# Selective scan with its states dealt out as a Latin square, and a quarter of du*B made by TensorE and ScalarE

## The chip, the core and the metric

The kernel runs on one core of a Trainium2 chip. A core has several engines, each with its own instruction stream, worked off in program order: TensorE (PE in the profile) multiplies matrices into PSUM, VectorE (DVE) and GpSimd (POOL) work elementwise, ScalarE (ACT) evaluates `func(scale * x + bias)`, and SyncE (SP) issues transfers (DMA) between the chip's memory and the on-chip memory SBUF. The engines meet only through semaphores: an instruction starts when what it reads has been written and what it overwrites has been read.

The metric is the device time of one execution in microseconds. The time before is 8235.37 us, the median of three runs (8234.65 to 8238.02).

## The reference

Two layers over images of 128 channels and 128 x 128 pixels, four of them, in float32. The first is a Mamba block over the L = 16384 pixels of an image as a sequence, the second a filter in the frequency domain. The change is in the first, around its recurrence:

```python
u     = silu(conv(x_in) + conv_b)                 # 256 channels
dt, Bm, Cm = split(u @ x_proj_w.T, [8, 24])       # 8, 16 and 16 columns
delta = softplus(dt @ dt_proj_w.T + dt_proj_b)    # 256 channels
A     = -exp(A_log)                               # 256 channels x 16 states

def step(h, inp):                                 # over the 16384 pixels
    d_t, B_t, C_t, u_t = inp
    dA = exp(d_t[:, :, None] * A)
    h  = h * dA + d_t[:, :, None] * B_t[:, None, :] * u_t[:, :, None]
    y  = einsum('bds,bs->bd', h, C_t)
    return h, y

y = (ys + u * D) * silu(z)
out = y @ out_proj_w.T                            # then group norm, silu, + x
```

There are 256 x 16 = 4096 recurrences per image, each over 16384 steps: h = h * dA + du*B, where du is delta * u. After it come a group normalisation with Silu and the residual, a small pooled network that yields four weights per image, and the second layer.

## The kernel before

**Chunks, units, pairs.** A chunk k is T = 512 pixels of one image; there are 4 x 32 = 128. A partition holds one channel and one of four states: 32 channels (DG) x 4 states (SQ) = 128 partitions. A chunk's recurrences are then 2 halves of channels (j, 128 channels each) x 4 groups of states (g) x 4 groups of channels in the half (m), 32 tiles of 128 x 512. A unit is four of these tiles: before, one (j, g) with all four m. A unit is worked in two pairs, so a chunk has NP = 16 pairs.

**Loads.** B, C, delta and du come out of the chip's memory in that layout: B and C by repeating four rows of states over 32 channels, delta and du by repeating every channel over four states.

```python
def bc_load():
    for q, tag in enumerate("BC"):
        t = d[tag] = p2.tile([P, NG, T], ...)
        for g in range(NG):
            nc.sync.dma_start(out=t[:, g, :],
                in_=d["bc"][q, g * SQ : (g + 1) * SQ, :].partition_broadcast(DG))
def dt_act():                                    # delta, and its store
    delta = d["dn"] = p1.tile([P, NH, T], ...)
    for j in range(NH):
        nc.scalar.activation(delta[:, j, :], ps["dt", j], AF.Softplus, bias=...)
    for j in range(NH):
        nc.sync.dma_start(out=d["dd"][0, j * P : (j + 1) * P, :], in_=delta[:, j, :])
def du_pool(j):                                  # du, and its store
    if j == 0:
        d["dun"] = p1.tile([P, NH, T], ...)
    du = d["dun"][:, j, :]
    nc.gpsimd.tensor_tensor(du, d["dn"][:, j, :], d["u"][:, j, :], ALU.mult)
    nc.sync.dma_start(out=d["dd"][1, j * P : (j + 1) * P, :], in_=du)
```

**The unit.** GpSimd makes du*B for all four tiles in one instruction (`dbu`). ScalarE makes two exponentials per pair into PSUM (`exps`). VectorE scans them; the product with C is VectorE's for most second pairs, GpSimd's for most first pairs (`scans`). TensorE adds the states up into y, one PSUM bank for each half (`sums`).

```python
def dbu(u):
    hb = d["hb", j, g] = p4.tile([P, ND, T], ...)
    nc.gpsimd.tensor_tensor(hb, d["du", j],
        d["B"][:, g : g + 1, :].to_broadcast([P, ND, T]), ALU.mult)
def exps(n):
    da = d["da", j, g, m] = psd.tile([P, 2, T], ...)             # PSUM, 2 buffers
    for q in range(2):
        nc.scalar.activation(da[:, q, :], d["delta", j][:, m + q, :], AF.Exp, scale=...)
def scans(n):
    dve = m > 0 or (j == 0 and g == NG - 1)
    h = da if dve else p2.tile([P, 2, T], tag="h", ...)
    for q in range(2):
        nc.vector.tensor_tensor_scan(h[:, q, :], da[:, q, :], hb[:, m + q, :], init, ALU.mult, ALU.add)
    eng = nc.vector if dve else nc.gpsimd
    eng.tensor_tensor(hb[:, m : m + 2, :], h, cr, ALU.mult)      # cr: C of group g
    nc.scalar.copy(last, h[:, :, T - 1])                         # state for the next chunk
def gate(j):                                                     # in post(k)
    nc.vector.tensor_mul(d["yg"][:, j, :], d["zs"][:, j, :], d["y", j])
```

**The schedule.** It is written by hand: a slot is one pair, and every piece of a chunk has a slot and a phase. Slot 0 is the pair with which a chunk's scans begin, slots below 0 lie in the chunk before, and all pieces of a slot are issued in the order of the phases.

```python
(-9, "pe", load), (-7, "pe", h1_mm), (-6, "act", h1_act), (-5, "pe", xm_mm), (-4, "act", xm_act),
(-3, "pe", z_mm), (-2, "act", z_act), (-1, "pe", cv_mm 0), (0, "pe", cv_mm 1),
(2, "act", silu_act), (3, "pe", xd_mm), (4, "act", xd_act), (5, "pe", dt_mm), (5, "act", bc_load),
(6, "act", dt_act), (7, "pool", du_pool 0), (8, "pool", du_pool 1),
(9, "act", rep_load 0), (16, "pe", rep_load 1),                  # delta and du, repeated
...
(26, "dve", gate 0), (34, "dve", gate 1), (35, "pe", o_mm), (36, "act", o_act), (50, "dve", o_stats)
# these are moved 16 slots forward, as a chunk's inputs are made during the chunk before
# pair n: exps in slot n - 1, scans in n; unit of pair n: dbu in n - 2, sums in n + 3
for phase in ("sums", "pe", "exps", "act", "pool", "dbu", "scans", "dve", "end"):
```

Since the slots are counted modulo 16, gate 0 stands in slot 10 and gate 1 in slot 2 of the following chunk; `cv_mm` (the convolution, 8 accumulating matmuls over two slots) stands in slots 15 and 0.

While one image is scanned, the image before is normalised (slots 2, 7 and 8 of half its chunks) and pooled (slots 4, 7 and 8 of the other half). For the last image both come after the loop, alone, and then the second layer follows.

Of the kernel before, what the change touches and what calls it, by code (L numbers as in the profile page):

```python
# [26 lines left out]
F32 = mybir.dt.float32  # L27
AF = mybir.ActivationFunctionType
ALU = mybir.AluOpType
# [14 lines left out]
def kernel(ctx: ExitStack, tc: tile.TileContext, a: dict, out: bass.AP):  # L44
# [41 lines left out]
    wdt = const("wdt", [R, DI], a["dt_wT"])  # L86
    cwb = const("cwb", [P, KC, DI], a["conv_wT"].partition_broadcast(P))
    bdt = col("dt_b")
# [29 lines left out]
    wck = cpool.tile([P, KC, DI], F32, tag="wck", name="wck")  # L118
    for t in range(KC):
        nc.vector.tensor_mul(wck[:, t, :], win[:, 0:DI], cwb[:, t, :])  # L120

# [15 lines left out]
def block0(tc, s):  # L137
    nc, B, NCH, NH, NS, NG, ND, R, NX, KC, HALO, C, L, NF, DI = (
        s.nc, s.B, s.NCH, s.NH, s.NS, s.NG, s.ND, s.R, s.NX, s.KC, s.HALO, s.C, s.L, s.NF, s.DI,
    )  # L140
    with ExitStack() as ctx:
        def pool(name, bufs, **kw):
# [3 lines left out]
        p2 = pool("p2", 2)  # L146
        p4 = pool("p4", 4)
        tiny = pool("tiny", 2)
        dbc = pool("dbc", 2, space=DRAM)
        dob = pool("dob", 2, space=DRAM)  # L150
        psp = pool("psp", 2, space=PSUM)
        psy = pool("psy", 1, space=PSUM)
        psd = pool("psd", 2, space=PSUM)

# [16 lines left out]
        def pre(k):  # L171
# [7 lines left out]
            def load():  # L179
                xt = d["xt"] = p2.tile([P, T], F32, tag="xt", name=f"xt_{k}")  # L180
                nc.sync.dma_start(out=xt, in_=s.xflat[b, :, i * T : (i + 1) * T])
# [60 lines left out]
            def bc_load():  # L242
                for q, tag in enumerate("BC"):
                    t = d[tag] = p2.tile([P, NG, T], F32, tag=f"r{tag}", name=f"r{tag}_{k}")
                    for g in range(NG):
                        nc.sync.dma_start(
                            out=t[:, g, :], in_=d["bc"][q, g * SQ : (g + 1) * SQ, :].partition_broadcast(DG)
                        )

# [7 lines left out]
            def dt_act():  # L257
# [4 lines left out]
                for j in range(NH):  # L262
                    nc.sync.dma_start(out=d["dd"][0, j * P : (j + 1) * P, :], in_=delta[:, j, :])

            def du_pool(j):
                if j == 0:
                    d["dun"] = p1.tile([P, NH, T], F32, tag="du", name=f"du_{k}")
                du = d["dun"][:, j, :]
                nc.gpsimd.tensor_tensor(du, d["dn"][:, j, :], d["u"][:, j, :], ALU.mult)  # L269
                nc.sync.dma_start(out=d["dd"][1, j * P : (j + 1) * P, :], in_=du)  # L270

            def rep_load(j):
# [8 lines left out]
                (-3, "pe", z_mm), (-2, "act", z_act), (-1, "pe", partial(cv_mm, 0)), (0, "pe", partial(cv_mm, 1)),  # L281
                (2, "act", silu_act), (3, "pe", xd_mm), (4, "act", xd_act), (5, "pe", dt_mm), (5, "act", bc_load),
                (6, "act", dt_act), (7, "pool", partial(du_pool, 0)), (8, "pool", partial(du_pool, 1)),
                (9, "act", partial(rep_load, 0)), (16, "pe", partial(rep_load, 1)),
            ]

        def dbu(u):

            k, r = divmod(u, NH * NG)
            j, g = divmod(r, NG)  # L290
            d = st[k]
            hb = d["hb", j, g] = p4.tile([P, ND, T], F32, tag="hb", name=f"hb_{k}_{j}_{g}")
            nc.gpsimd.tensor_tensor(hb, d["du", j], d["B"][:, g : g + 1, :].to_broadcast([P, ND, T]), ALU.mult)  # L293

        def pair(n):

            k, r = divmod(n, NP)
            u, m = divmod(r, ND // 2)
            j, g = divmod(u, NG)
            return k, j, g, 2 * m  # L300

        def exps(n):
            k, j, g, m = pair(n)
            d = st[k]
            da = d["da", j, g, m] = psd.tile([P, 2, T], F32, tag="da", name=f"da_{k}_{j}_{g}_{m}")
            for q in range(2):
                c = (j * NG + g) * ND + m + q
                nc.scalar.activation(da[:, q, :], d["delta", j][:, m + q, :], AF.Exp, scale=s.amat[:, c : c + 1])  # L308

        def scans(n):  # L310

            k, j, g, m = pair(n)
            d = st[k]
            hb = d["hb", j, g]
            da = d.pop(("da", j, g, m))
            dve = m > 0 or (j == 0 and g == NG - 1)
            last = d["last", j, g, m] = tiny.tile([P, 2], F32, tag=f"st{j}_{g}_{m}", name=f"st_{k}_{j}_{g}_{m}")
            h = da if dve else p2.tile([P, 2, T], F32, tag="h", name=f"h_{k}_{j}_{g}_{m}")
            for q in range(2):
                init = 0.0 if k % NCH == 0 else st[k - 1]["last", j, g, m][:, q : q + 1]  # L320
                nc.vector.tensor_tensor_scan(h[:, q, :], da[:, q, :], hb[:, m + q, :], init, ALU.mult, ALU.add)  # L321
            cr = d["C"][:, g : g + 1, :].to_broadcast([P, 2, T])
            eng = nc.vector if dve else nc.gpsimd
            eng.tensor_tensor(hb[:, m : m + 2, :], h, cr, ALU.mult)  # L324
            nc.scalar.copy(last, h[:, :, T - 1])  # L325

        def sums(u):

            k, r = divmod(u, NH * NG)
            j, g = divmod(r, NG)  # L330
            d = st[k]
            if g == 0:
                y = d["y", j] = psy.tile([P, T], F32, tag=f"y{j}", name=f"y_{k}_{j}")
                nc.tensor.matmul(y, s.diag[:, j, :], d["u"][:, j, :], start=True, stop=False)
            y = d["y", j]
            for q in range(ND):
                nc.tensor.matmul(  # L337
                    y[q * DG : (q + 1) * DG, :], s.sel, d["hb", j, g][:, q, :], start=False, stop=g == NG - 1
                )

        def post(k):

            b, i = divmod(k, NCH)
            d = st[k]

            def gate(j):
                if j == 0:
                    d["yg"] = p1.tile([P, NH, T], F32, tag="yg", name=f"yg_{k}")
                nc.vector.tensor_mul(d["yg"][:, j, :], d["zs"][:, j, :], d["y", j])

            def o_mm():
                d["po"] = psum(f"o_{k}")
                for j in range(NH):
                    nc.tensor.matmul(d["po"], s.wo[:, j, :], d["yg"][:, j, :], start=j == 0, stop=j == NH - 1)  # L354

            def o_act():
                if i == 0:
                    stats[b] = tiny.tile([P, NCH, 6], F32, tag="stats", name=f"stats_{b}")
                    outs[b] = dob.tile([C, L], F32, tag="ob", name=f"ob_{b}")
                d["o"] = p2.tile([P, T], F32, tag="o", name=f"o_{k}")  # L360
                nc.scalar.copy(d["o"], d["po"])
                nc.sync.dma_start(out=outs[b][:, i * T : (i + 1) * T], in_=d["o"])

            def o_stats():
                nc.vector.bn_stats(stats[b][:, i, :], d["o"])
                st.pop(k - 1, None)

            return [
                (26, "dve", partial(gate, 0)), (34, "dve", partial(gate, 1)), (35, "pe", o_mm), (36, "act", o_act),
                (50, "dve", o_stats),  # L370
            ]
# [40 lines left out]
        def finish(b):  # L412
# [12 lines left out]
            def norm_load(i):  # L425
                xr = g["x", i] = p4.tile([P, T], F32, tag="xr", name=f"xr_{b}_{i}")
                o = g["o", i] = p4.tile([P, T], F32, tag="of", name=f"of_{b}_{i}")
                nc.sync.dma_start(out=xr, in_=s.xflat[b, :, i * T : (i + 1) * T])
                nc.sync.dma_start(out=o, in_=outs[b][:, i * T : (i + 1) * T])
# [29 lines left out]
            def agg_load(i):  # L459
                x1 = g["x1", i] = p4.tile([P, T], F32, tag="xr", name=f"x1_{b}_{i}")  # L460
                nc.sync.dma_start(out=x1, in_=s.x1flat[b][:, i * T : (i + 1) * T])
# [40 lines left out]
            for i in range(NCH):  # L502
                c = (2 + i // 2) * NP
                r = i % 2
                todo += [
                    (c - 3 + r, "pe", partial(norm_load, i)), (c + 2, "act", partial(norm_act, i)),
                    (c + 7, "pe", partial(norm_mm, i)), (c + 8, "dve", partial(norm_dve, i)),
                ]
# [22 lines left out]
        for n in range(n_chunks * NP):  # L531
            todo[n - 1, "exps"].append(partial(exps, n))
            todo[n, "scans"].append(partial(scans, n))
            if n % 2 == 0:
# [4 lines left out]
        with tc.manual_schedule():  # L539
            for n in range(min(slots), max(slots) + 1):  # L540
                for phase in ("sums", "pe", "exps", "act", "pool", "dbu", "scans", "dve", "end"):
                    for f in todo[n, phase]:
                        f()
# [196 lines left out]
```

## Time and profile before

The profile is one execution taken by the hardware profiler. Its page gives, for the span of 8235.9 us:

| engine | busy us | share | instructions |
|---|---|---|---|
| VectorE | 7666.4 | 93% | 6640 |
| GpSimd | 7519.2 | 91% | 2500 |
| TensorE, matmuls | 6064.7 | 74% | 20532 |
| ScalarE | 5263.0 | 64% | 9495 |
| transfers, mean of 16 engines | | 46% | |

By stretches of the span, busy microseconds in each:

| stretch, us | VectorE | GpSimd | ScalarE | TensorE | what runs |
|---|---|---|---|---|---|
| 4000 to 5000 | 954 | 970 | 673 | 714 | scan loop |
| 7000 to 7300 | 204 | 156 | 130 | 154 | end of the loop, normalisation of the last image |
| 7500 to 8236 | 713 | 457 | 321 | 716 | second layer |

A row of the page's costliest groups reads: line, engine, operation, output <- inputs by the program's names, partitions x elements of output and input, count | busy us in total, mean ns of one | idle time of the engine just ahead of them, and what ended most of it. In the names, hb is du*B and later h*C, da the exponential, rB, rC, rdu and rdelta the repeated tiles, st the carried state, dd and bc the buffers in the chip's memory. The view of waits has one row for each kind of wait: who waited <- for whom: us in total, how many times, the longest. Matmuls of float32 stand as two records each.

### The profile page before, as it was taken

Reading aid. Unit: us, or ns where it says so; the run is one execution under the profiler, and the core shown is the slowest. Engines: PE = TensorE matmul, PEld = TensorE weight load, DVE = VectorE, ACT = ScalarE, POOL = GpSimd, SP = SyncE. Lnnn points to the kernel's source line nnn. Section 1 sums busy time; section 2 is a strip of 40 time slices with the busy share of each in tenths; the row PEclk is TensorE's granted clock in tenths of the full one; section 3 lists DMA queues with packets and bytes.
Section 4 is the critical chain, followed back from the end, with each engine's and each line's share of the span. In section 5 each row is a group of like instructions: output and inputs, shape, how many; then the busy total and the mean of one; then the engine's idle time right before and its main releaser. Section 6 shows DMA issues by size and latency. Waiting matters only on the chain.

```text
span 8235.9 us, 73103 instructions
## 1 busy us (share of the span) xinstructions
PE 6064.7 (74%) x20532; PEld 2229.5 (27%) x20532; DVE 7666.4 (93%) x6640; ACT 5263.0 (64%) x9495; POOL 7519.2 (91%) x2500
## 2 busy tenths in 40 slices
PE   6677777776777777777777767777777777569999
PEld 1121121111111222221111222221111222138888
DVE  6999999999999999999999999999999999839999
ACT  5666666666666676676666666676666766534444
POOL 7999999999999999999999999999999999716665
PEclk8777777778988878888888888888888888779999
DMA  4444444444454444445454444445454444454443
GB/s 151 141 141 153 144 152 137 146 153 160 163 175 156 168 155 162 147 161 173 153 176 165 152 165 155 160 149 175 163 172 168 151 150 165 135 171 115 115 124 93
DMA packets 838679, 1257.45 MB, mean 153 GB/s; under 512 B 78200, under 2 KB 276864, under 8 KB 838272
## 3 DMA queue, kind: packets, MB, share of 16 engines
q1 hardware_dynamic: 835760, 1252.43, 46.0%
q8 instruction: 162, 2.65, 0.1%
q14 instruction: 245, 2.01, 0.1%
q10 hardware_dynamic: 2512, 0.36, 0.0%
HBM read 1009.22 MB, written 243.27 MB: 152 GB/s over the span
## 4 chain that ended last, share of the span: by engine, by line
DVE 36%; issue 25%; POOL 20%; ACT 14%; DMA 2%; PE 2%; SPq 0%; DVEq 0%; POOLq 0%; ACTq 0%
DVE da L321 15%; POOL hb L293 10%; DVE h L321 8%; POOL hb L324 7%; ACT da L308 5%; DVE hb L324 3%; DVE wb L590 3%; POOL du L269 2%; ACT L308 2%; ACT L226 2%; ACT u L226 2%; ACT zs L227 1%; DVE im L617 1%; DVE ii L620 1%; DVE ot L644 1%
## 5 line engine op out<-in xcount | busy, mean ns | idle before, releaser
L293 POOL TENSOR_TENSOR hb<-rdu,rB 128x2048 f32<-128x2048 f32 x1024 | 4640.6, 4532 | 16.4 <-DMA rdu<-dd 16.4
L321 DVE TENSOR_TENSOR_SCAN da<-da,st,hb 128x512 f32<-128x512 f32 x2232 | 2862.5, 1282 | 42.0 <-ACT da L308 2.5
L308 ACT ACTIVATE da<-rdelta,amat 128x512 f32<-128x512 f32 x4096 | 2831.9, 691 | 102.8 <-ACT st L325 0.2
L337 PE MATMUL y<-hb,sel 128*32 128x512 f32 x8192 | 1648.3, 735 | 1299.3 <-POOL hb L324 1140.0
L321 DVE TENSOR_TENSOR_SCAN h<-da,st,hb 128x512 f32<-128x512 f32 x1736 | 2127.8, 1267 | 220.4 <-ACT st L325 109.7
L324 POOL TENSOR_TENSOR hb<-h,rC 128x1024 f32<-128x1024 f32 x896 | 2111.3, 2356 | 103.6 <-DVE h L321 101.3
L324 DVE TENSOR_TENSOR hb<-da,rC 128x1024 f32<-128x1024 f32 x1152 | 1410.3, 1224 | 51.9
L325 ACT COPY st<-da 128x2 f32<-128x2 f32 x1152 | 184.4, 160 | 1930.3 <-DVE hb L324 1929.6
L221 PE MATMUL pp_cv<-xm,wck 128*128 128x512 f32 x2048 | 981.5, 634 | 56.8 <-ACT zs L215 56.8
L337 PEld LDWEIGHTS y<-hb,sel 128*32 128x32 f32 x8192 | 219.1, 116 | 2552.6 <-POOL hb L324 1788.4
L221 PEld LDWEIGHTS pp_cv<-xm,wck 128*128 128x128 f32 x2048 | 404.0, 203 | 658.6 <-issue 455.3
L616 POOL TENSOR_TENSOR re<-sq 128x520 f32<-128x520 f32 x64 | 84.8, 1325 | 469.1 <-ACT sq L614 469.0
L186 PE MATMUL pp_h<-xt,w 128*128 128x512 f32 x512 | 349.5, 807 | 193.8 <-DMA xt<-in_x 80.3
L354 PE MATMUL pp_o<-yg,wo 128*128 128x512 f32 x512 | 370.6, 864 | 126.7 <-ACT u L226 126.7
L210 PE MATMUL pp_z<-xm,win 128*128 128x512 f32 x512 | 358.8, 839 | 72.7 <-ACT xm L204 72.7
L269 POOL TENSOR_TENSOR du<-delta,u 128x512 f32<-128x512 f32 x256 | 320.2, 1274 | 60.1 <-ACT delta L261 60.1
L253 PE MATMUL pp_dt<-xd,wdt 8*128 8x512 f32 x512 | 313.0, 739 | 83.2 <-ACT xd L238 83.2
L196 PE MATMUL pp_xm<-h,w 128*128 128x512 f32 x512 | 308.2, 733 | 60.1 <-ACT h L191 60.1
L308 ACT ACT_TABLE_LOAD x261 | 334.9, 1283 | 2.9
L325 ACT COPY st<-h 128x2 f32<-128x2 f32 x896 | 171.6, 192 | 246.0 <-DVE h L321 235.4
L437 PE MATMUL pp_xr<-xr,ident 128*128 128x512 f32 x256 | 210.8, 970 | 158.3 <-DMA xr<-in_x 71.0
L590 DVE SCALAR_TENSOR_TENSOR wb<-ft,wts,wb 128x1040 f32<-128x1040 f32 x192 | 296.8, 1547 | 4.4
(107 smaller groups left out, 7378.9 us busy)
## 6 DMA issues: line engine op xcount, KB each, us to landing
rdelta<-dd SPq DMA_DIRECT2D x1024, 256.0 KB, 3.6
rdu<-dd SPq DMA_DIRECT2D x1024, 256.0 KB, 4.7
rB<-bc SPq DMA_DIRECT2D x512, 256.0 KB, 3.9
rC<-bc SPq DMA_DIRECT2D x512, 256.0 KB, 5.0
dd<-delta SPq DMA_DIRECT2D x256, 256.0 KB, 4.9
dd<-du SPq DMA_DIRECT2D x256, 256.0 KB, 3.4
ft<-in_filt_w SPq DMA_DIRECT2D x64, 520.0 KB, 7.1
xt<-in_x SPq DMA_DIRECT2D x128, 256.0 KB, 5.2
```

The lines of the kernel that those rows point to most:

```text
L186: nc.tensor.matmul(ps["h", j], s.w1[:, j * P : (j + 1) * P], d["xt"], start=True, stop=True)
L210: nc.tensor.matmul(ps["z", j], w, d["xm"][:, HALO:], start=True, stop=True)
L221: nc.tensor.matmul(ps["cv", j], w, d["xm"][:, t : t + T], start=t == 0, stop=t == KC - 1)
L269: nc.gpsimd.tensor_tensor(du, d["dn"][:, j, :], d["u"][:, j, :], ALU.mult)
L293: nc.gpsimd.tensor_tensor(hb, d["du", j], d["B"][:, g : g + 1, :].to_broadcast([P, ND, T]), ALU.mult)
L308: nc.scalar.activation(da[:, q, :], d["delta", j][:, m + q, :], AF.Exp, scale=s.amat[:, c : c + 1])
L321: nc.vector.tensor_tensor_scan(h[:, q, :], da[:, q, :], hb[:, m + q, :], init, ALU.mult, ALU.add)
L324: eng.tensor_tensor(hb[:, m : m + 2, :], h, cr, ALU.mult)
L325: nc.scalar.copy(last, h[:, :, T - 1])
L337: nc.tensor.matmul(y[q * DG : (q + 1) * DG, :], s.sel, d["hb", j, g][:, q, :], start=False, stop=g == NG - 1)
L354: nc.tensor.matmul(d["po"], s.wo[:, j, :], d["yg"][:, j, :], start=j == 0, stop=j == NH - 1)
L590: nc.vector.scalar_tensor_tensor(wb, ft[:, f], s.wts[b][0:H, f : f + 1], wb, ALU.mult, ALU.add)
```

## The change

**Latin square.** A unit is now (j, r) with a rotation r: its place p holds state group p of channel group (p - r) mod 4. So every unit holds each group of states once and each group of channels once, and after four rotations all sixteen combinations have come. What is made differently for state group 0 is thus one tile of every unit, the first.

**du*B of group 0.** It leaves GpSimd. TensorE turns du so that pixels lie on partitions; there B is one number per partition, so ScalarE multiplies by it as its scale operand (`bt_act`, 16 products of 128 x 256 per chunk); TensorE turns the result back, four 128 x 128 blocks per unit, into PSUM (`dbu_turn`), where the scan reads it. The exponential of that tile goes to SBUF. GpSimd makes the other three tiles in one or two instructions, and B of group 0 isn't loaded in repeated form.

**Who makes the product with C.** GpSimd for all first pairs, and for one second pair (j = 1, r = 2) of every odd chunk; VectorE for the rest.

**Room.** du is written over delta, and the gated y over z; y has one PSUM bank instead of two (the other takes the turned du); the pools of four 128 x 512 buffers in normalisation and pooling have two or three; the input xt has one.

**Order.** The phases get "turn" at their head and "gate" ahead of "scans"; gates and the additions of the normalisation move there.

```diff
             def bc_load():
                 for q, tag in enumerate("BC"):
-                    t = d[tag] = p2.tile([P, NG, T], F32, tag=f"r{tag}", name=f"r{tag}_{k}")
-                    for g in range(NG):
...
+                    t = d[tag] = p2.tile([P, NG - 1 + q, T], F32, tag=f"r{tag}", name=f"r{tag}_{k}")
+                    for g in range(1 - q, NG):
...
+            def xd_turn():
+                ps["xt"] = turned(f"xdt_{k}")
+                for t in range(NT):
+                    nc.tensor.transpose(ps["xt"][:, t, 0:NX], d["xd"][:, t * P : (t + 1) * P], s.ident[0:NX, 0:NX])
+            def xd_turn_act():
+                d["xdt"] = p1.tile([P, NT, NX], F32, tag="xdt", name=f"xdt_{k}")
+                nc.scalar.copy(d["xdt"], ps["xt"][:, :, 0:NX])
+            def du_turn(h):
+                ps["dut"] = turned(f"dut_{k}_{h}")
+                for t in range(2):
+                    for j in range(NH):
+                        at = (2 * h + t) * P
+                        nc.tensor.transpose(ps["dut"][:, 2 * t + j, :], d["dn"][:, j, at : at + P], s.ident)
+            def bt_act(h, n0, n1):
+                if h == n0 == 0:
+                    d["bt"] = p2.tile([P, NT, NH * ND, DG, SQ], F32, tag="bt", name=f"bt_{k}")
+                for n in range(n0, n1):
+                    t, q = divmod(n, SQ)
+                    src = ps["dut"][:, 2 * t : 2 * t + 2, :].rearrange("p j (g d) -> p (j g) d", d=DG)
+                    nc.scalar.activation(d["bt"][:, 2 * h + t, :, :, q], src, AF.Copy,
+                        scale=d["xdt"][:, 2 * h + t, R + q : R + q + 1])
             def du_pool(j):
-                if j == 0:
-                    d["dun"] = p1.tile([P, NH, T], F32, tag="du", name=f"du_{k}")
-                du = d["dun"][:, j, :]
-                nc.gpsimd.tensor_tensor(du, d["dn"][:, j, :], d["u"][:, j, :], ALU.mult)
+                du = d["dn"][:, j, :]
+                nc.gpsimd.tensor_tensor(du, du, d["u"][:, j, :], ALU.mult)
...
-                (6, "act", dt_act), (7, "pool", partial(du_pool, 0)), (8, "pool", partial(du_pool, 1)),
-                (9, "act", partial(rep_load, 0)), (16, "pe", partial(rep_load, 1)),
+                (5, "act", bc_load), (6, "act", dt_act), (7, "act", xd_turn_act), (7, "pool", partial(du_pool, 0)),
+                (7, "pool", partial(du_pool, 1)), (8, "turn", partial(du_turn, 0)), (9, "act", partial(rep_load, 0)),
+                (8, "pool", partial(bt_act, 0, 0, 3)), (9, "act", partial(bt_act, 0, 3, 4)),
+                (10, "act", partial(bt_act, 0, 4, 7)), (11, "act", partial(bt_act, 0, 7, 8)),
+                (12, "turn", partial(du_turn, 1)), (12, "act", partial(bt_act, 1, 0, 3)),
+                (13, "act", partial(bt_act, 1, 3, 4)), (14, "act", partial(bt_act, 1, 4, 8)),
+                (16, "pe", partial(rep_load, 1)),
...
+            p = 1                                   # in dbu: places 1 to 3 of the unit
+            while p < NG:
+                m = place(r, p)                     # (p - r) % ND
+                n = min(NG - p, ND - m)
+                nc.gpsimd.tensor_tensor(
+                    hb[:, p : p + n, :], d["du", j][:, m : m + n, :], d["B"][:, p - 1 : p - 1 + n, :], ALU.mult)
+                p += n
...
+        def dbu_turn(n):
+            ps = d["ps", j, r, p] = psd.tile([P, 2, T], F32, tag="da", name=f"ps_{k}_{j}_{r}_{p}")
+            if p == 0:
+                for t in range(NT):
+                    src = d["bt"][:, t, j * ND + place(r, 0), :, :].rearrange("p d s -> p (d s)")
+                    nc.tensor.transpose(ps[:, 0, t * P : (t + 1) * P], src, s.ident)
...
-            dve = m > 0 or (j == 0 and g == NG - 1)
+            dve = p > 0 and not (k % 2 and j == 1 and r == 2)
...
-                y = d["y", j] = psy.tile([P, T], F32, tag=f"y{j}", name=f"y_{k}_{j}")
+                y = d["y", j] = psy.tile([P, T], F32, tag="y", name=f"y_{k}_{j}")
...
-                (26, "dve", partial(gate, 0)), (34, "dve", partial(gate, 1)), (35, "pe", o_mm), (36, "act", o_act),
+                (26, "gate", partial(gate, 0)), (34, "gate", partial(gate, 1)), (36, "pe", o_mm), (36, "act", o_act),
...
-                x1 = g["x1", i] = p4.tile([P, T], F32, tag="xr", name=f"x1_{b}_{i}")
+                x1 = g["x1", i] = p2.tile([P, T], F32, tag="xr", name=f"x1_{b}_{i}")
...
+            todo[n - 1, "turn"].append(partial(dbu_turn, n))
...
-                for phase in ("sums", "pe", "exps", "act", "pool", "dbu", "scans", "dve", "end"):
+                for phase in ("turn", "sums", "pe", "exps", "act", "pool", "dbu", "gate", "scans", "dve", "end"):
```

## The prediction

> **What bounds the kernel now.** I read the page's busy shares first, then the costliest groups, then the waits of VectorE between 1000 and 7000 us, then the timelines of single engines across one chunk.
>
> ```profile
> PE 6064.7 (74%) x20532; PEld 2229.5 (27%) x20532; DVE 7666.4 (93%) x6640; ACT 5263.0 (64%) x9495; POOL 7519.2 (91%) x2500
> ...
> L293 POOL TENSOR_TENSOR hb<-rdu,rB 128x2048 f32<-128x2048 f32 x1024 | 4640.6, 4532 | 16.4 <-DMA rdu<-dd 16.4
> L321 DVE TENSOR_TENSOR_SCAN da<-da,st,hb 128x512 f32<-128x512 f32 x2232 | 2862.5, 1282 | 42.0 <-ACT da L308 2.5
> L308 ACT ACTIVATE da<-rdelta,amat 128x512 f32<-128x512 f32 x4096 | 2831.9, 691 | 102.8 <-ACT st L325 0.2
> ...
> L324 POOL TENSOR_TENSOR hb<-h,rC 128x1024 f32<-128x1024 f32 x896 | 2111.3, 2356 | 103.6 <-DVE h L321 101.3
> L324 DVE TENSOR_TENSOR hb<-da,rC 128x1024 f32<-128x1024 f32 x1152 | 1410.3, 1224 | 51.9
> ...
> L269 POOL TENSOR_TENSOR du<-delta,u 128x512 f32<-128x512 f32 x256 | 320.2, 1274 | 60.1 <-ACT delta L261 60.1
> ```
>
> The scan loop starts at 57.7 us and its last product ends near 7160 us on VectorE's timeline: 7103 us for 128 chunks, **55.5 us a chunk**. GpSimd's three groups give 8 x 4.53 + 7 x 2.36 + 2 x 1.27 = 55.3 us; the starts in its timeline lie about 0.05 us closer than the durations, so some 54.4 us of 55.5. VectorE waits little; the view of its waits (total, times, longest) gives for 6000 us:
>
> ```profile
> DVE h L321 <- ACT st L325: 109.6, 60, 2.2
> DVE h L321 <- POOL hb L293: 79.8, 153, 0.8
> DVE rstd L404 <- ACT rstd L401: 4.5, 3, 1.5
> DVE da L321 <- ACT da L308: 2.5, 3, 0.8
> ```
>
> The four add up to 196 us in 108 chunks, 1.8 us a chunk, so VectorE needs 55.5 - 1.8 = **53.7 us** of work. It checks: in its timeline a pair whose product VectorE makes takes 3.77 us from start to start, a pair whose product goes to GpSimd 2.365; 9 x 3.77 + 7 x 2.365 = 50.5, and gates, statistics and the normalisation's additions make some 3.2. Both engines are bound, GpSimd a little more. The 1.8 us at line 321 come after the Silu stage, where two table loads hold ScalarE.
>
> **What the Trainium skill says.** "SBUF — State Buffer", section Who interferes with whom: a VectorE instruction with two SBUF inputs contends with a GpSimd instruction that reads SBUF, one with a single SBUF input doesn't. The new first scan takes the exponential from SBUF but du*B from PSUM, so it still has one. The trace agrees: scans of that kind last 1267 to 1282 ns next to a GpSimd that is 91% busy. "ScalarE: Activation LUTs", section What ACT_TABLE_LOAD costs, has 186 ns + 0.833 ns an element, 93 ns more for a pointer operand, 93 ns of overlap between neighbours, and a table load of 1283 ns. The trace has 1283 for the load, and 578 to 580 (no pointer) and 673 to 691 (one) for 512 elements, 15 to 35 below the formula. "TensorE: Matmul & The Clock Gate", Part 4, gives about 275 ns for a 128x128 turn within a kernel. The kernel before has no turn; its 128x128 products have rows of 282 to 287 ns that overlap in time (205 us busy for 1024 of 283).
>
> **The change, engine by engine, per chunk.**
>
> *GpSimd.* du*B falls from 8 x 2048 columns to 8 x 1536. Durations for 512, 1024 and 2048 columns (1274, 2356, 4532) lie on a line, so 1536 takes about 3.44. Rotations 0 and 1 need one instruction each, rotations 2 and 3 two each (512 and 1024): over both halves 4 x 3.44 + 4 x (1.27 + 2.36) = 28.3 instead of 36.3. Products go from 7 to 8.5 on average (every first pair, and one second pair of odd chunks): 20.0 instead of 16.5. With du that is 50.9, some 49.8 in starts: **4.5 us less**.
>
> *VectorE.* 1.5 pairs lose their product: 1.5 x (3.77 - 2.365) = **2.1 us less, 51.6 us**. This is the new floor; held everywhere it would save 3.9 us a chunk.
>
> *ScalarE.* 16 products of 256 elements and one copy of 160. From rows of 376 ns (260 elements, no pointer) plus about 0.1 for the pointer I take 0.48 each, about 0.39 from start to start: 6.2 + 0.3 = **6.5 us more**. In the stretch from 1000 to 7000 us it was about 68% busy, 37.5 us a chunk; it becomes 44. That is below the floor, but it lies in slots 8 to 14, beside h1, xm and z.
>
> *TensorE.* 32 turns for du*B, 8 of du, 4 of xd: 44 a chunk, at 0.15 to 0.28 us **7 to 12 us** more. It was 72% busy, 40 us, with real gaps; it fits in sum. But its matmuls run in program order, and turns now stand first in it.
>
> *DMA.* One of four B loads less: 256 KB of some 9 MB a chunk (160 GB/s over 55.5 us). Hidden before, hidden after.
>
> *After the loop.* The last batch is normalised and pooled with nothing beside it (7160 to 7358 us). Normalising goes 8.1 us a pair because the queue issues the next loads only after the last stores; fewer buffers change little. Pooling took 40 us for 32 tiles with four buffers, 1.25 us each. With two, a buffer's round is a landing (3.0 us by the DMA view) and a matmul (1.0): 2.0 us each, **about 20 us more** once.
>
> **New waits.** Here I walked through one chunk by slots; a slot pair takes VectorE 6.2 us.
>
> 1. du is now written over delta, so GpSimd must wait until delta has been stored. All transfers of dd between 2000 and 3000 us took a median 4.5 us to land. Softplus is ready some 3.5 and 4.2 us into slot 6, so du can start only near 8.2 and ends near 10.7, that is 4.5 us into slot 8. TensorE turns it by 5.1, ScalarE makes three products and then the exponential for slot 10 by about 7.6, where VectorE wants it at 6.2 (7.5 where normalisation adds 1.3 us to slot 8). Stall 0 to 1.4 us, average **0.8**. GpSimd's own idle time there, 3.8 us, fits in its slack.
> 2. The turn for the next chunk's first unit heads TensorE's slot 15 and needs the last bt product. ScalarE makes that after exp (1.4), z (1.1) and four products (1.6), about 4.3 us into slot 14, 0.5 to 1.9 us into slot 15 with what it lags. Then come the turns (0.6), the sums (1.1), the two convolutions (7.1, measured) and only after them the turns and sums of slot 17, near 12 us. The gate of the second half now stands before the scans of slot 18 and wants those sums at 3.78 + 6.15 = 9.9. Stall up to **2 to 2.7 us**. The kernel before had its convolutions done before that slot and the gate after its scans. In exchange ScalarE's Silu wait (109.6 us in 108 chunks, 1.0 a chunk) goes, since VectorE arrives later.
> 3. Small ones (softplus, GpSimd's hb): 0.4 us; the one on hb, 0.7 before, shrinks, as GpSimd no longer lags.
>
> The walk takes the unlucky order at each step: 0.8 + 2.4 + 0.4 = 3.6, a period of 55.2, which is no gain. If the new waits cost only what the old ones did (1.8), the period is 53.4. The rotation, the alternation of one product by the parity of the chunk, and the bt products in pieces of three, one and four look fitted to a running kernel, so I lean towards the better half and choose 2.8: **54.4 us**. Then 57.7 + 3 (one more link before the first scan) + 128 x 54.4 + the 1076 us from 7160 to the end + 20 = 8120, and with rounding of these parts I say **8125 us**, 1.3% less.
>
> **Rivals.** *The engines' sums decide.* Period 52 to 53: 7810 to 7940. For it: both bound engines lose work and GpSimd had no slack. Against: four engines now stand between 44 and 52 us, each in program order. *TensorE becomes the link that ends last.* Every unit needs four turns that wait for a scan of two slots before, behind the convolutions: period 55 to 57, 8200 to 8450. For it: 7.13 us of convolution in one piece in TensorE's timeline, against 6.2 us of VectorE's two slots. Against: TensorE had gaps of 1 to 2 us around nearly every group. *ScalarE becomes it*, if products that write every fourth element run slower than 0.39: at 0.6 it is 3.4 us more in slots that have no slack; half or all of it on top of 54.4 makes 8340 to 8550. No group of the kernel before writes so on ScalarE, so nothing in its profile decides this.
>
> **Range and chances.** A stall of 1.3 to 4.5 us a chunk around 2.8 gives 7930 to 8340. Faster by 2% means below 8071, a stall under 2.4: 0.42. Slower by 2% means above 8400, a stall near 5: 0.10. The rest, 0.48.
>
> **What would show it.** Right: the GpSimd group of hb splits into 512, 1024 and 1536 columns with 1.27, 2.36 and 3.44 us and GpSimd's busy time falls by about 560 us; VectorE's falls by about 270; ScalarE's rises by some 830; gates wait for y of TensorE, and du waits for the DMA dd<-delta. Wrong: gates that don't wait (then the first rival, near 7900), bt products well off 0.48 us, turns far above 0.28, scans longer than 1.29 us, or pooling after the loop still at 1.25 us a tile.

## The result: 5.7% slower

The changed kernel takes 8704.4 us (median of 4 runs, 8693.3 to 8726.0), the kernel before 8236.7 beside it: a ratio of 1.057 (95% interval 1.055 to 1.059). The prediction said 8125 us, with a range up to 8340.

The page after, in the busy shares and the groups that answer to those shown before, with the gate (line 413), the new product (line 293), the turns (line 360) and the convolution (line 225) added:

```profile
PE 6551.2 (75%) x26164; PEld 2881.2 (33%) x26164; DVE 7425.3 (85%) x6448; ACT 6204.1 (71%) x11671; POOL 6957.5 (80%) x3204
...
L340 POOL TENSOR_TENSOR hb<-rdu,rB 128x1536 f32<-128x1536 f32 (+2 forms) x1536 | 3606.0, 2363 | 10.2 <-DMA rdu<-dd 10.2
L389 POOL TENSOR_TENSOR hb<-h,rC 128x1024 f32<-128x1024 f32 x1088 | 2567.9, 2362 | 517.6 <-DVE h L387 512.3
...
L360 PE MATMUL ps<-ident,bt 128*128 128x128 f32 x4096 | 812.1, 329 | 1415.6 <-DVE h L387 1359.5
L293 ACT ACTIVATE bt<-pt_dut,xdt 128x256 f32<-128x256 f32 x2048 | 1201.0, 709 | 518.9 <-PE pt_dut L282 518.9
...
L225 PE MATMUL pp_cv<-xm,wck 128*128 128x512 f32 x2048 | 1044.0, 667 | 0.0
L299 POOL TENSOR_TENSOR delta<-delta,u 128x512 f32<-128x512 f32 x256 | 317.9, 1263 | 668.1 <-DMA dd<-delta 604.1
...
L413 DVE TENSOR_TENSOR zs<-zs,y 128x512 f32<-128x512 f32 x256 | 175.7, 686 | 588.3 <-PE y L403 587.9
```

Work fell as foreseen: VectorE by 241 us, GpSimd by 562. But neither is above 85% busy any more. The last columns say what stands in the gaps: VectorE's gates waited 588 us for y, GpSimd's du waited 604 us for the store of delta. The page's view of the chain of work that ended last, as shares of the span, first before and then after, shows the same shift: TensorE went from 2% to 27%, and the convolution alone is 11%.

```profile
DVE 36%; issue 25%; POOL 20%; ACT 14%; DMA 2%; PE 2%; SPq 0%; DVEq 0%; POOLq 0%; ACTq 0%
```

```profile
PE 27%; DVE 27%; ACT 17%; DMA 9%; POOL 8%; issue 8%; SPq 3%; DVEq 0%; POOLq 0%; ACTq 0%
PE pp_cv L225 11%; DVE h L387 8%; DVE ps L387 7%; ACT ps L372 6%; PE y L403 6%; DMA dd<-delta 6%; POOL hb L340 4%; ACT bt L293 4%; DVE hb L389 3%; PE ps L360 3%; DVE wb L655 3%; SPq L251 3%; POOL hb L389 2%; POOL delta L299 2%; PE pp_xd L236 1%
```

The scan loop runs from 64.0 to about 7615 us, **59.0 us a chunk** instead of 55.5. VectorE's waits between 1000 and 7000 us:

```profile
DVE zs L413 <- PE y L403: 446.4, 163, 4.7
DVE h L387 <- ACT ps L372: 91.8, 81, 2.3
DVE h L387 <- ACT st L390: 86.4, 64, 1.8
DVE of L505 <- PE pp_xr L501: 44.5, 42, 1.5
DVE h L387 <- POOL hb L389: 43.3, 22, 2.6
```

With the two largest of the smaller rows (rstd 13.7, of 7.1) that is 733 us in 101 chunks, 7.3 us a chunk instead of 1.8. Split by gate, over 67 chunks of VectorE's timeline from 2000 to 6000 us, the first gate waits 1.65 us a chunk on average (39 of 67 times), the second 2.67 (every time).

Why the second gate waits is seen in TensorE's timeline where one chunk passes to the next (start, us, instruction, count, idle before and its releaser):

```profile
4064.32 0.63 PE L360 MATMUL ps<-ident,bt 128*128 128x128 f32 x4 [3.61 <-DVE h L387]
4064.88 1.93 PE L403 MATMUL y<-hb,sel 128*32 128x512 f32 x8
4066.75 7.88 PE L225 MATMUL pp_cv<-xm,wck 128*128 128x512 f32 x16
4074.46 0.60 PE L360 MATMUL ps<-ident,bt 128*128 128x128 f32 x4
4074.99 1.06 PE L403 MATMUL y<-hb,sel 128*32 128x512 f32 x8
```

TensorE stands idle for 3.6 us until VectorE's scan of two slots before has freed the PSUM tile, then turns, adds up, works 7.7 us on the convolution, and only then gets to the next unit's turns and the sums for the gate. VectorE and ScalarE at the same place:

```profile
4076.12 0.69 DVE L413 TENSOR_TENSOR zs<-zs,y 128x512 f32<-128x512 f32 x1 [2.04 <-PE y L403]
...
4075.10 0.69 ACT L372 ACTIVATE ps<-rdelta,amat 128x512 f32<-128x512 f32 x1 [3.94 <-PE ps L360]
```

ScalarE was held as well: the second exponential of a first pair goes into the PSUM tile of the turns, and waited 3.9 us for them.

The first gate waits behind another stop of TensorE. The turns of du stand at the head of slot 8, ahead of the sums that this gate needs; they wait for GpSimd's du, which waits for the store of delta. In the timeline from 2000 to 6000 us, TensorE's last stop before each of the first gate's waits is at these turns. One chunk, TensorE and then VectorE:

```profile
4103.33 0.47 PE L282 MATMUL pt_dut<-ident,delta 128*128 128x128 f32 x1 [3.55 <-POOL delta L299]
4104.55 0.90 PE L282 MATMUL pt_dut<-ident,delta 128*128 128x128 f32 x3 [0.75 <-POOL delta L299]
4105.25 1.06 PE L360 MATMUL ps<-ident,bt 128*128 128x128 f32 x4
4106.24 1.94 PE L403 MATMUL y<-hb,sel 128*32 128x512 f32 x8
...
4108.24 0.69 DVE L413 TENSOR_TENSOR zs<-zs,y 128x512 f32<-128x512 f32 x1 [0.63 <-PE y L403]
```

### The profile page after: what moved, and what is told of

Read it like the earlier page. It is cut to its first block, busy times and chain, and to the rows that moved or that the text cites. A ratio compares the mean times of both kernels' runs of the same rounds, so it can differ in the third digit from the quotient of the medians.

```text
span 8724.2 us, 87385 instructions
## 1 busy us (share of the span) xinstructions
PE 6551.2 (75%) x26164; PEld 2881.2 (33%) x26164; DVE 7425.3 (85%) x6448; ACT 6204.1 (71%) x11671; POOL 6957.5 (80%) x3204
## 3 DMA queue, kind: packets, MB, share of 16 engines
q8 instruction: 210, 3.44, 0.2%
## 4 chain that ended last, share of the span: by engine, by line
PE 27%; DVE 27%; ACT 17%; DMA 9%; POOL 8%; issue 8%; SPq 3%; DVEq 0%; POOLq 0%; ACTq 0%
PE pp_cv L225 11%; DVE h L387 8%; DVE ps L387 7%; ACT ps L372 6%; PE y L403 6%; DMA dd<-delta 6%; POOL hb L340 4%; ACT bt L293 4%; DVE hb L389 3%; PE ps L360 3%; DVE wb L655 3%; SPq L251 3%; POOL hb L389 2%; POOL delta L299 2%; PE pp_xd L236 1%
## 5 line engine op out<-in xcount | busy, mean ns | idle before, releaser
L340 POOL TENSOR_TENSOR hb<-rdu,rB 128x1536 f32<-128x1536 f32 (+2 forms) x1536 | 3606.0, 2363 | 10.2 <-DMA rdu<-dd 10.2
L372 ACT ACTIVATE ps<-rdelta,amat 128x512 f32<-128x512 f32 x3072 | 2126.4, 692 | 653.3 <-PE ps L360 586.4
L387 DVE TENSOR_TENSOR_SCAN ps<-ps,st,hb 128x512 f32<-128x512 f32 x1856 | 2375.8, 1280 | 45.3
L360 PE MATMUL ps<-ident,bt 128*128 128x128 f32 x4096 | 812.1, 329 | 1415.6 <-DVE h L387 1359.5
L293 ACT ACTIVATE bt<-pt_dut,xdt 128x256 f32<-128x256 f32 x2048 | 1201.0, 709 | 518.9 <-PE pt_dut L282 518.9
L387 DVE TENSOR_TENSOR_SCAN h<-da,st,ps 128x512 f32<-128x512 f32 x992 | 1263.8, 1274 | 276.2 <-ACT ps L372 125.6
L387 DVE TENSOR_TENSOR_SCAN h<-ps,st,hb 128x512 f32<-128x512 f32 x1120 | 1398.8, 1258 | 3.0 <-ACT ps L372 3.0
L360 PEld LDWEIGHTS ps<-ident,bt 128*128 128x128 f32 x4096 | 560.2, 166 | 1953.4 <-issue 1734.6
L389 DVE TENSOR_TENSOR hb<-ps,rC 128x1024 f32<-128x1024 f32 x960 | 1175.6, 1225 | 32.7
L225 PE MATMUL pp_cv<-xm,wck 128*128 128x512 f32 x2048 | 1044.0, 667 | 0.0
L372 ACT ACTIVATE da<-rdelta,amat 128x512 f32<-128x512 f32 x1024 | 752.1, 734 | 3.1
```

The source lines that it names most:

```text
L225: nc.tensor.matmul(ps["cv", j], w, d["xm"][:, t : t + T], start=t == 0, stop=t == KC - 1)
L293: nc.scalar.activation(d["bt"][:, 2 * h + t, :, :, q], src, AF.Copy, scale=d["xdt"][:, 2 * h + t, R + q : R + q + 1])
L340: nc.gpsimd.tensor_tensor(hb[:, p : p + n, :], d["du", j][:, m : m + n, :], d["B"][:, p - 1 : p - 1 + n, :], ALU.mult)
L360: nc.tensor.transpose(ps[:, 0, t * P : (t + 1) * P], src, s.ident)
L372: nc.scalar.activation(da, d["delta", j][:, m, :], AF.Exp, scale=s.amat[:, c : c + 1])
L387: nc.vector.tensor_tensor_scan(h[:, q, :], da, b, init, ALU.mult, ALU.add)
```

## The experiments

Theory A: TensorE's program order, with the convolution in one piece between two units' turns. Theory B: ScalarE's strided products. Theory C: the store of delta that du waits for. Theory D: each of these waits would be replaced by the next.

### Products in runs of 32

```diff
-  d["bt"] = p2.tile([P, NT, NH * ND, DG, SQ], ...)    ... d["bt"][:, 2 * h + t, :, :, q]
+  d["bt"] = p2.tile([P, NT, NH * ND, SQ, DG], ...)    ... d["bt"][:, 2 * h + t, :, q, :]
```

> The products bt are written as 32 neighbouring elements instead of every fourth one; du*B of group 0 then reaches the wrong state partitions, the work is otherwise the same. Theory B (ScalarE's strided stores are the cause: 709 ns against the 480 foreseen): a product falls to about 480 ns, the slots 8 to 14 get their slack back, 3 us a chunk, about 8300 us. Theory A (TensorE's program order, with the convolutions behind the last turn, is the cause): the products become cheaper all the same, but the turns come only 0.5 to 1 us earlier and the gates still wait 3 us a chunk, about 8550 us.

Measured 8610 us, ratio 1.045 (1.044 to 1.047): 94 us less. The group of the products:

```profile
L293 ACT ACTIVATE bt<-pt_dut,xdt 128x256 f32<-128x256 f32 x2048 | 840.2, 470 | 520.4 <-PE pt_dut L282 520.4
```

470 ns instead of 709, so the stride is what the product pays for. But the gates still wait 1.41 and 1.99 us a chunk: theory A's figure was the nearer one. Theory B is real and small.

### Gates behind the scans

```diff
-  (26, "gate", partial(gate, 0)), (34, "gate", partial(gate, 1))
+  (26, "dve", partial(gate, 0)), (34, "dve", partial(gate, 1))
```

> Both gates go back behind the scans of their slot, as in the kernel before. If the place of the gate is the cause, its wait of 4.3 us a chunk hides behind 2.4 us of scans twice, about 8250 us. Theory A: the scans of the same slot need turns and exponentials that stand behind the same convolutions, so the wait moves from the gate to the scan, about 8620 us.

8684 us, ratio 1.055 (1.053 to 1.056): 20 us less, and VectorE's waits from 1000 to 7000 us have moved:

```profile
DVE h L387 <- ACT st L390: 344.2, 206, 4.1
DVE h L387 <- ACT ps L372: 214.1, 126, 4.2
```

The gate is only where VectorE meets TensorE's lateness first. Behind it, scans wait for exponentials. These are still late: ScalarE waits 464.4 us for the turns in this stretch, against 472.9 in the change.

### The first half of the convolution ahead of the turns

```diff
-  (-1, "pe", partial(cv_mm, 0))
+  (-1, "head", partial(cv_mm, 0))          # "head": a new phase, ahead of "turn"
```

> The first half of the convolution is issued ahead of the turns of slot 15, where TensorE waits 3.6 us with nothing to do. Theory A: turns and sums of slot 17 come about 3.5 us earlier, the wait of the second gate (2.7 us a chunk) nearly goes, the Silu wait of ScalarE grows by some 0.5 us: about 8430 us. Theory B: TensorE isn't what ends last, within 60 us of 8704.

8967 us, ratio 1.089 (1.087 to 1.091): 262 us *more*. It was meant to fill TensorE's 3.6 us of idle time. TensorE's timeline shows why it didn't:

```profile
4027.77 5.33 PE L225 MATMUL pp_cv<-xm,wck 128*128 128x512 f32 x8 [3.97 <-ACT zs L219]
4032.94 0.60 PE L360 MATMUL ps<-ident,bt 128*128 128x128 f32 x4
```

The convolution needs a PSUM buffer that ScalarE frees by copying z, which ScalarE does behind four products of slot 14. So TensorE waited 4 us for that, and the turns, which VectorE needs, came 5 us later. The wait at the second gate is gone and the first gate's stays (116 us from 2000 to 6000 us), but 360 us of waits for `ACT st` stand at the scans of the same stretch. Theory A predicted this edit wrongly, but the run fits it: what holds up the turns holds up VectorE, here by 262 / 128 = 2.0 us a chunk net.

### A buffer of its own for du

```diff
-  du = d["dn"][:, j, :]
-  nc.gpsimd.tensor_tensor(du, du, d["u"][:, j, :], ALU.mult)
+  du = d["dun"][:, j, :]
+  nc.gpsimd.tensor_tensor(du, d["dn"][:, j, :], d["u"][:, j, :], ALU.mult)   # delta shares h1's buffer
```

> du gets a buffer of its own (delta shares one with h1), so GpSimd needn't wait for the store of delta: its wait of 4.4 us a chunk at that line goes. Theory C (the store of delta is the cause): du, its turn and the products come 3 to 4 us earlier, the wait of the first gate (1.65 us a chunk) goes, about 8500 us, and if slots 9 to 15 then run ahead of VectorE, the second gate's as well, about 8350. Theory A: only the first gate's wait goes, 8500 to 8550 us.

8458 us, ratio 1.027 (1.026 to 1.029): 246 us less. GpSimd's wait for the store is gone and the first gate doesn't wait once in 69 chunks. The second gate does, 3.21 us a chunk, more than before. Theory C holds for the first gate alone.

### The convolution in two slots

```diff
-  (-1, "pe", partial(cv_mm, 0)), (0, "pe", partial(cv_mm, 1))
+  (-1, "pe", partial(cv_mm, 0)), (1, "pe", partial(cv_mm, 1))
```

> The second half of the convolution moves from slot 0 to slot 1, behind the turns of slot 17 and the sums that the second gate needs; nothing else changes. Theory A (the 7.8 us of convolution in one piece between two units' turns hold the second gate): its wait of 2.7 us a chunk goes and about 8380 us remain, with the first gate's wait as it was. Theory D (VectorE would only wait at the next place, the exponentials behind Silu, since silu comes later too): within 80 us of 8704.

8269 us, ratio 1.004 (1.003 to 1.005): **436 us less from moving four matmuls by one slot**. VectorE's waits from 1000 to 7000 us:

```profile
DVE h L387 <- ACT st L390: 135.6, 108, 2.0
DVE h L387 <- ACT ps L372: 82.6, 99, 2.3
DVE zs L413 <- PE y L403: 66.9, 67, 3.2
```

The gates went from 446 to 67 us. That is more than the second gate's share: the first gate's wait fell from 1.65 to 0.26 us a chunk too. ScalarE's wait for the turns in the same stretch fell too, from the first of these lines (the change) to the second (this run):

```profile
ACT ps L372 <- PE ps L360: 472.9, 116, 6.3
```

```profile
ACT ps L372 <- PE ps L360: 169.0, 129, 2.9
```

A faster TensorE is not the reason. The granted clock was 0.87 here and 0.84 in the change, but the convolutions were busy for 1067.3 us here and for 1044.0 there. Theory D is out as a full account: of the 380 us that the gates lost, only 49 came back at `ACT st`. Theory A carries most of the loss.

### Both together

> The split convolution and the own buffer of du together. Theories A and C are two separate links: the gains add, 8704 - 246 - 340, about 8110 us, faster than the kernel before. Theory D: about 8400, as with the own buffer alone.

8155 us, ratio 0.990 (0.989 to 0.991): faster than the kernel before. The two gains are 436 and 246 alone and 549 together, so they overlap by some 130 us; they are not quite separate links. That this lands near the 8125 us forecast is no confirmation: the forecast was for a kernel without these two edits.

### The same with products in runs of 32

> Own buffer of du and split convolution, with the products bt written as 32 neighbouring elements in the order (state, channel), so that du*B of group 0 reaches the wrong partitions (the loads keep their order). Theory B, late: now that the other waits are gone, ScalarE is what VectorE waits for (2.4 us a chunk of waits for it in the middle of the loop), and 16 x 0.24 = 3.8 us less work there makes about 8000 us. If those waits are Silu's table loads alone, within 50 us of 8155.

8080 us, ratio 0.981 (0.979 to 0.982): 76 us less than with strided products, between the two expectations. ScalarE loses 284 us of busy time for it, so three quarters were beside other work. The largest of VectorE's waits that remain is that at `ACT st`, 137 us in 109 chunks, once a chunk behind Silu's table loads; no run here touched it.

### Runs of 32 that reach the right partitions

For that, all tiles must have partitions (state, channel):

```diff
-  in_=rows.partition_broadcast(DG)                       # B, C
+  in_=rows.rearrange("s (o t) -> s o t", o=1).to_broadcast([SQ, DG, T])
-  in_=replicated(d["dd"][q, r : r + DG, :])              # delta, du
+  in_=d["dd"][q, r : r + DG, :].partition_broadcast(SQ)
```

> Partitions (state, channel) instead of (channel, state) for everything: the products bt are written in runs of 32 neighbours and reach the right partitions; the loads of delta and du repeat a block of 32 channels four times, those of B and C repeat each state over 32 partitions. If the loads don't mind, the time is that of the run with contiguous products alone, 8610 us. If the loads become slower in this order (a reason to have stayed with (channel, state)), more, up to the 8704 of the change.

10602 us, ratio 1.287 (1.285 to 1.289). Against the run with contiguous products alone (8610 us) only the order of the partitions differs, and with it the loads. Two stretches in which this kernel loads du, then one in which the change loads delta and du beside other transfers (stretch and length, busy us and counts of PE, PEld, DVE, ACT and POOL, granted clock, share of the DMA engines, GB/s):

```profile
4017.00:4027.00 10.00, 7.43 (x32) 2.71 (x26) 9.17 (x9) 8.77 (x21) 10.00 (x6) 0.98 0.27 102
4036.00:4048.00 12.00, 9.98 (x36) 3.81 (x28) 9.23 (x9) 4.15 (x9) 9.72 (x4) 0.92 0.26 99
```

```profile
4045.00:4053.00 8.00, 6.67 (x31) 2.27 (x29) 7.58 (x7) 7.83 (x17) 8.00 (x4) 0.83 0.92 323
```

The loads, of 256 KB each in both kernels, arrive at 100 GB/s in the first two stretches, with 26% of the DMA engines busy; in the third it is 323 GB/s and 92%. "DMA: Bandwidth & Descriptors" of the Trainium skill, section Why a DMA increments its semaphore by 16 and not by 1, says that a transfer is spread over the largest number of engines up to 16 that divides the slowest dimension of both sides. Here that dimension is 4 (the states, or the copies of a channel), and 4 of 16 is 25%. The measured share agrees; no run varied that dimension by itself. It is a reason to keep (channel, state) and pay with strided stores.

The same order in the mended kernel, with the pooling of the next section:

> Split convolution, own buffer of du, partitions (state, channel) with contiguous products, and the pooling's loads dealt over five buffers instead of two. If ScalarE is close behind in the run before (it loses 16 x 0.24 = 3.8 us of work a chunk here), 7950 us; if it isn't, only the pooling's 25 us: 8085 us.

10056 us, ratio 1.221 (1.219 to 1.223). It has the same slow loads, so it says nothing on ScalarE.

### Five buffers for pooling

```diff
-  x1 = g["x1", i] = p2.tile([P, T], F32, tag="xr", ...)
+  n, tag = ((2, "xr"), (3, "o"))[i % 2]
+  x1 = g["x1", i] = p2.tile([P, T], F32, tag=tag, ..., bufs=n)
```

> The run with the own buffer of du and the split convolution (8155 us), and the pooling's loads dealt over five buffers instead of two. After the loop the pooling should go back from about 70 to about 40 us: 8125 us. If it isn't the buffers that slowed the pooling, 8155 us.

8124 us, ratio 0.986 (0.985 to 0.988): 31 us less than without. The wait for the last pooling fell from 69.9 us in the change to 37.6.

### One more product for GpSimd

```diff
-  dve = p > 0 and not (k % 2 and j == 1 and r == 2)
+  dve = p > 0 and not (j == 1 and r == 2)
```

> As the run with five pooling buffers, and GpSimd makes the second product of (j = 1, r = 2) in every chunk instead of every other one. GpSimd waits 4.7 us a chunk for VectorE, so it has room: VectorE loses 0.7 us a chunk. If VectorE's own work sets the pace, 90 us less, about 8040 us; if waits do, 0 to 40 us less.

**8030 us, ratio 0.975 (0.973 to 0.976)**, the fastest version here and 95 us less than the run before it. Its busy shares:

```profile
PE 6240.2 (78%) x26164; PEld 2742.5 (34%) x26164; DVE 7327.6 (91%) x6384; ACT 6217.9 (77%) x11671; POOL 7111.4 (89%) x3268
```

VectorE's busy time fell by 85 us against the run before it (7412.9 there) and the whole by 95, while VectorE's waits from 1000 to 7000 us did not fall (350 us there, 381 here). So its own work set the pace, as the expectation's first case had it.

### The Latin square alone

The kernel before, with units by rotation and nothing else:

```diff
-  nc.gpsimd.tensor_tensor(hb, d["du", j], d["B"][:, g : g + 1, :].to_broadcast([P, ND, T]), ALU.mult)
+  while p < NG:                                # from p = 0
+      m = (p - g) % ND; n = min(NG - p, ND - m)
+      nc.gpsimd.tensor_tensor(hb[:, p : p + n, :], d["du", j][:, m : m + n, :], d["B"][:, p : p + n, :], ALU.mult)
+      p += n
```

> The kernel before with the Latin square alone: units by rotation, GpSimd makes all four tiles of du*B (28 instructions a chunk instead of 8... with the instruction counts of the rotations, 1, 2, 2 and 2 for each half, 14 instead of 8), nothing goes to TensorE and ScalarE, and buffers and phases stay. Six more starts of about 0.19 us each make 1.1 us a chunk on GpSimd, which bounds the kernel before: about 8370 us. If the square costs in some other way (operands that are no longer repeated, another order of partitions), more; if GpSimd's starts are hidden, 8235.

8308 us, ratio 1.009 (1.007 to 1.010): 71 us more. (Of the two counts in the expectation, 14 instead of 8 is the right one.) GpSimd's busy time rose by 112 us for 768 more instructions, 0.15 us each; some of that was hidden, and a start costs less than the 0.19 us foreseen. No cost of the square beyond its instructions shows.

## Why the prediction was wrong, step by step

**The savings were right.** du*B takes 1276, 2366 and 3447 ns for 512, 1024 and 1536 columns (foreseen 1.27, 2.36, 3.44). GpSimd lost 562 us (560), VectorE 241 (270). Scans last 1258 to 1280 ns, those with the exponential in SBUF and du*B in PSUM 1274, so no contention shows there. A period of 59.0 less 7.3 of waits is 51.7 us of work, the foreseen floor.

**The step that failed is the sum of the new waits.** The walk had 0.8 + 2.4 + 0.4 = 3.6 us; measured were 7.3. The signs that the prediction named did come: gates wait for y of TensorE, and du waits for the store of delta. The mechanism was largely right, and these terms of the sum were mis-sized:

- *ScalarE's waits, taken as gone:* the walk let Silu's wait of 1.0 us a chunk vanish, since VectorE would arrive later. At `ACT st` 86.4 us remain in 101 chunks, 0.9 us a chunk. New is the wait at `ACT ps`, 91.8 us, another 0.9. Together 1.8 us stand where the walk had zero, half of what it missed. The exchange exists but is small: with the convolution split the gates hardly wait, and the wait at `ACT st` is 135.6 us. The late turns hold ScalarE too (3.9 us in the lines shown); how much of the 1.8 us comes from that, no run separates.
- *The first gate:* foreseen 0.8, measured 1.65. The cause was seen (with its own buffer of du the wait is zero), the path was not. The walk went from du's turns through three products to the exponential of slot 10. In the trace the turns of du hold back TensorE's sums, and the gate waits for those. Shorter products alone left 1.41 us.
- *The second gate:* foreseen up to 2 to 2.7, measured 2.67. The mechanism is the one described, and the split convolution shows it; that the size fits is partly luck. The walk took 7.1 us for the convolution, which was the fastest case: the line below gives 981.5 / 128 = 7.7 us a chunk before, and the one after 1044.0 / 128 = 8.2. The split also took 1.4 us from the first gate of each chunk, a reach that the walk did not have; by which links is not shown.
- *Small ones:* 0.4 foreseen. The normalisation's additions, hb and the reciprocal together wait 1.1 us.

```profile
L221 PE MATMUL pp_cv<-xm,wck 128*128 128x512 f32 x2048 | 981.5, 634 | 56.8 <-ACT zs L215 56.8
```

**Then a choice made it worse.** The walk gave 55.2 us a chunk, no gain. The prediction leaned from 3.6 to 2.8 because pieces of the change "look fitted to a running kernel", which no view of the profile supports. The walk alone would have said 57.7 + 3 + 128 x 55.2 + 1076 + 20, about 8220, still far below 8704: the mis-sized terms weigh more than the choice.

**ScalarE's products** cost 0.71 us instead of 0.48, and three in a row 1.7 us, some 0.5 from start to start, where 0.39 was foreseen and the third rival had 0.6. The prediction named this as what nothing in the profile could decide. "SBUF — State Buffer" of the Trainium skill, section Door 1: The DMA port swizzle, says that SBUF has lines of 16 bytes and that each access to a new line pays a penalty. Every fourth float32 is a new line, and the runs agree with that reading: 709 ns with the stride, 470 without. ScalarE's busy time rose by 941 us where some 830 were foreseen. The stride's weight in the total is 94 us, so the third rival was real but was not the cause.

**TensorE's turns** cost what was foreseen, 0.15 to 0.28 us: 812.1 us for 4096 of them, 0.20 each. Most groups of four took 0.60 to 0.63 us, about a third 1.04 to 1.11. The 275 ns that the prediction quotes from "TensorE: Matmul & The Clock Gate" of the Trainium skill, Part 4, are given there for bf16; these turns are float32.

**The second rival** had the link that ends last: units whose turns stand behind the convolutions in TensorE's order. It isn't the amount of TensorE's work (75% busy). Its period of 55 to 57 us was still short of 59.0, since the first gate and ScalarE's waits come on top.

**After the loop** pooling took 70 us; foreseen were 60, and five buffers took most of it back.

What stays open is how the remaining 1.2 us a chunk behind Silu's table loads could be hidden, and by which links the two main mends overlap by 130 us.

## What to carry to other kernels

When work moves to an engine with slack, look at what stands *ahead* of it in that engine's program order: here 7.7 us of convolution between two units' turns cost 436 us, and moving four matmuls by one slot gave it back. A buffer saved by writing in place turns a transfer that nobody waited for into a link of the chain (246 us). In a schedule by slots, follow a delay through every engine that touches the same tile before letting one wait replace another.

## What the runs showed of the hardware

- ScalarE's stores of every fourth float32 take 709 ns for 128 x 256, in runs of 32 they take 470.
- Four 128x128 turns of float32 in a row took 0.60 to 0.63 us in most groups and 1.04 to 1.11 in about a third; over all 4096 of the change it is 0.20 us each.
- Loads of 256 KB with 4 as their outermost size ran at 100 GB/s, with 26% of the DMA engines busy; a stretch of loads with 32 outermost, beside other transfers, at 323 GB/s with 92%.
- A GpSimd product costs the same whether an operand is repeated or plain: 2048 columns take 4532 ns with B repeated (the kernel before) and 4522 with plain operands (the Latin square alone).
